# Where the load of layer 1's first value weights stands in SyncE's queue, in a two-layer attention kernel

## The chip, the cores and the metric

The kernel runs on one core of a Trainium2 chip. The metric is the device time of one execution in microseconds (us). Everything is fp32.

## What is computed

The input is 4 images of 16x16 pixels with 1024 channels, that is, 1024 tokens of 1024 features. Two layers follow each other, of which only the seam matters here:

```python
x = x + _L0_conv_ref(_gn(x), ...)        # layer 0: linear attention, content and position parts
t = _to_tokens(x)
t = t + _L1_attn_ref(_ln_t(t), ...)      # layer 1: qkv = einsum('btc,oc->bto', ln, W_attn) + b_attn, 16 heads
t = t + _L1_ffn_ref(_ln_t(t), ...)       # 8 gated experts
```

In layer 0 the content part and the position part add up to a matrix that is multiplied with the values: `Y = Yc + Yp`. The result is added to `x`, the tokens are normed over their features (`_ln_t`), and layer 1 starts with its value projection, which multiplies the normed tokens with the last third of `W_attn`.

## The kernel before

Tokens are worked on in 8 tiles of 128 (`NT`). At the seam the tiles come in the order of `tiles` (L569): second halves of the four images first (t = 1, 3, 5, 7), then the first halves (0, 2, 4, 6). The loop at L615 takes them one after the other, under a manual schedule, so that each engine runs its instructions in the order of the program. A step of it does this for tile i:

- `spread(i)` (L583): TensorE makes the content products of tile i+1 (`pc`, L444), VectorE adds them to the attention matrix `s` (L452); TensorE multiplies `s` with the values (`py`, L595) and VectorE adds that to `x` (L602).
- `layer_norm` (L184): VectorE takes the statistics, ScalarE writes the normed rows into one of three slots of `ln_rows` (L162).
- `turn_quarters(i - 2)` (L605): VectorE transposes the quarters of the tile before last into `ln1`, features on partitions (L179).
- `turn_by_rows` (L202): SyncE (SP) writes the normed rows to DRAM (L204), and four DMAs read them back as quarters (`quarters_of`, L174), which the transpose above takes two steps later.
- GpSimd adds `b_proj` to `x` and stores the rows to `x_rows` from its own queue (L629, L630).

The last two tiles don't go through DRAM: TensorE transposes them (`turn_on_pe`, L207). Tile 6 is normed in the loop, tile 7 (tile numbers are places in the order) after it.

All DMAs of SP stand in one queue in program order. Ahead of the loop stand 88 copies that move the position part from `two_T` to `s` (L479), and then the load of `w_v0`, 2 MB: the first half of layer 1's value weights, features by 512 columns. It is a `w_tile` (L115) from a pool of two buffers; the buffer that it gets held the key and value weights of layer 0 (`w_kv`). Its readers come after the loop: `first(0, 1)` and `first(0, 3)` on TensorE (L656, called at L710), and the sums `sums_v(0, nc.gpsimd)` on GpSimd (L152 to L155, called at L709). The second half, `w_v1` (L729), goes to the buffer of `ln_rows` once tile 7 has been transposed.

The value products that follow take the tiles of `ln1` by token: `first(0, 1)` and `first(0, 3)` need tiles 0 and 1 of the order, `first(0, 0)` (L719) needs tile 4 (t = 0), and `first(0, 2)` (L723) needs tile 5 (t = 2). PSUM has three banks with the tag `mm` and three with the tag `tr`; a product that takes a bank waits until the last reader of what was there has finished.

Of the kernel before, what the change touches and what calls it, by code (L numbers as in the profile page):

```python
# [40 lines left out]
C = 1024  # L41
# [16 lines left out]
HALF = 512  # L58
# [11 lines left out]
def kernel(  # L70
# [44 lines left out]
    def w_tile(name, *parts, home=None, queue=nc.sync):  # L115

        w = (home or wpool).tile([P, NC, HALF], F32, tag="w", name=name)
        at = 0
        for part in parts:
            n = part.shape[1]  # L120
            queue.dma_start(w[:, :, at : at + n], part.rearrange("(c p) n -> p c n", p=P))
            at += n
        return w
# [47 lines left out]
    def quarters_of(rows, row):  # L171

        for f in range(Q):
            nc.sync.dma_start(row[ts(f, 32), :, :], rows[:, f, :].rearrange("(g j) c -> j g c", j=32))  # L174
        return row
# [8 lines left out]
    def layer_norm(ln, t, on_pe=False):  # L184


        stats = small.tile([P, 2, 6], F32, tag="ln_stats", name=f"ln1_stats{t}")
        for j in range(2):
            nc.vector.bn_stats(stats[:, j, :], xs[t][:, ts(j, HALF)])
        mv = small.tile([P, 2], F32, tag="ln_mv", name=f"ln1_mv{t}")  # L190
        nc.vector.bn_aggr(mv, stats)
        rstd = small.tile([P, 1], F32, tag="ln_rstd", name=f"ln1_rstd{t}")
        inverse_root(rstd, mv[:, 1:2], EPS)
        if on_pe:
            less = small.tile([P, 1], F32, tag="ln_less", name=f"ln1_less{t}")
            nc.vector.scalar_tensor_tensor(less, mv[:, 0:1], -1.0, rstd, ALU.mult, ALU.mult)
            for j in range(2):
                nc.scalar.activation(ln[:, ts(j, HALF)], xs[t][:, ts(j, HALF)], AF.Identity, bias=less, scale=rstd)
            return
        normalised(ln, xs[t], mv[:, 0:1], rstd)  # L200

    def turn_by_rows(ln, t, quarters, turns):  # L202
        rows = turns.tile([P, Q, C // Q], F32, tag="rows", name=f"ln1_rows{t}")
        nc.sync.dma_start(rows.rearrange("n f c -> n (f c)"), ln)  # L204
        quarters_of(rows, quarters)
# [13 lines left out]
    with ExitStack() as layer0:  # L219
# [363 lines left out]
        def spread(i):  # L583
            b, nt = tiles[i]
            t = 2 * b + nt
            if i == 0:
                content(b, nt)
            if i + 1 < NT:
                content(*tiles[i + 1])
            for hp in range(2):  # L590
                py = mm(f"py{t}_{hp}")
                for hl in range(2):
                    bh = b * HEADS0 + 2 * hp + hl
                    for mh in range(2):
                        nc.tensor.matmul(  # L595
                            py[:, ts(hl, M)],
                            s0[:, mh, ts(nt, S2), :, bh].rearrange("p i j -> p (i j)"),
                            v_T[:, mh, ts(b, M)],
                            start=(mh == 0),
                            stop=(mh == 1),  # L600
                        )
                nc.vector.tensor_add(xs[t][:, ts(hp, HALF)], xs[t][:, ts(hp, HALF)], py)  # L602
            return t

        def turn_quarters(i):  # L605
            of, quarters = to_turn[i]
            turn(ln1[:, :, ts(of, P)], quarters)
# [2 lines left out]
            of[:, :C].rearrange("p (f c) -> p f c", f=Q)  # L610
            for of in (emb.rearrange("p c i j -> p (c i j)"), s_w.rearrange("p a c n -> p (a c n)"))
        ]
        w_v = [w_tile("w_v0", W_attnT[:, 2 * C : 2 * C + HALF])]
        in_order.enter_context(tc.manual_schedule())
        for i in range(NT - 1):  # L615
            t = spread(i)
            quarters = None
            if i < NT - 2:
                if i < NT - 4:
                    quarters = spare[i % 2]  # L620
                else:
                    quarters = late.tile([P, Q, C // Q], F32, tag="xg", name=f"ln1_quarters{t}")
            to_turn.append((t, quarters))
            layer_norm(ln_rows[:, i % 3, :], t, i >= NT - 2)
            if i >= 2:
                turn_quarters(i - 2)
            if i < NT - 2:
                turn_by_rows(ln_rows[:, i % 3, :], t, quarters, turns)
                nc.gpsimd.tensor_add(xs[t], xs[t], bp)  # L629
                nc.gpsimd.dma_start(x_rows[ts(t, P), :], xs[t])  # L630
            else:
                nc.sync.dma_start(x_rows[ts(t, P), :], xs[t])
# [1040 lines left out]
```

## Time and profile before

| What | Value |
|---|---|
| Time, median of 3 runs | 1248.14 us (1246.36 to 1249.39) |
| Time of the profiled execution | 1246.09 us |
| Its span | 1244.2 us |
| Busy: TensorE (PE) | 1221.8 us, 98% |
| Busy: VectorE (DVE) | 740.5 us, 60% |
| Busy: GpSimd (POOL) | 409.1 us, 33% |
| Busy: ScalarE (ACT) | 219.9 us, 18% |
| Mean granted TensorE clock | 0.995 |
| HBM read, written | 116.12 MB, 48.50 MB |

A page of the profile gives, for one execution, the busy time of each engine; the span in 40 equal slices, with the busy share in tenths (9 is 90% or more) and the granted clock of TensorE (PEclk) in tenths; the waits, each with what ended it; and the chain of work that ended last. A line of the timeline has the start in us, the duration in us, the engine, the line of the kernel, the operation with output and input and the number of instructions, and in brackets the idle time before it and what ended that. SPq stands for SyncE's queue of DMA issues: its duration is the issue, not the transfer. Times are us from the start of the span.

### The profile page before, as it was taken

What the parts mean: (1) busy time and instruction counts of PE and PEld (TensorE: products, weight loads), DVE (VectorE), ACT (ScalarE), POOL (GpSimd) and SP (SyncE); (2) the same over time, 40 slices, a digit from 0 to 9 for tenths busy, and PEclk for the clock granted to TensorE, in tenths of its full rate; (3) what the DMA queues carried; (4) which work ended last, traced back from release to release, by engine and by line L of the source; (5) the groups of instructions that cost most, each with busy time, mean ns of one, the idle gap of its engine ahead of it and who ended that gap; (6) DMA issues with size and microseconds to landing.
All of it is one profiled execution on the core that took longest, in us unless ns stands there. A gap on an engine that the chain in (4) does not pass through costs nothing.

```text
span 1244.2 us, 13333 instructions
## 1 busy us (share of the span) xinstructions
PE 1221.8 (98%) x4796; PEld 632.7 (51%) x4796; DVE 740.5 (60%) x1333; ACT 219.9 (18%) x514; POOL 409.1 (33%) x470
## 2 busy tenths in 40 slices
PE   9999999799999999999999999999999999999998
PEld 5445885578884444444444444444344434434443
DVE  5796636477332666657554866765656656565642
ACT  3310111121000222223121422110210111111110
POOL 0041341246000222222232115445552745363521
PEclk9999999899999999999999999999999999999999
DMA  9002025862202535353383657383856485656442
GB/s 350 20 1 85 1 52 155 261 210 69 68 1 68 155 103 160 107 169 107 102 288 117 209 203 255 72 234 91 240 126 176 103 235 154 155 129 190 100 84 54
DMA packets 94121, 169.77 MB, mean 136 GB/s; under 512 B 11968, under 2 KB 48848, under 8 KB 94048
## 3 DMA queue, kind: packets, MB, share of 16 engines
q1 hardware_dynamic: 75680, 112.68, 27.8%
q0 software_dynamic: 16144, 51.45, 17.3%
q10 hardware_dynamic: 2224, 4.72, 1.1%
q8 instruction: 40, 0.66, 0.2%
q14 instruction: 33, 0.27, 0.1%
HBM read 116.12 MB, written 48.50 MB: 132 GB/s over the span
## 4 chain that ended last, share of the span: by engine, by line
PE 73%; issue 13%; POOL 5%; DVE 3%; DMA 3%; SPq 2%; ACT 1%; POOLq 0%; DVEq 0%; ACTq 0%
PE p L1440 31%; PE pv L656 8%; PE po L897 6%; POOL s_q L854 5%; PE pq_pair L392 4%; PE left L1482 3%; PE pq L311 3%; PE pqk L656 3%; PE pk L423 2%; PE rest L1496 2%; PE pv L530 2%; PE pT L502 2%; SPq L479 1%; DMA s<-two_T 1%; DMA ln_rows<-ln_rows 1%
## 5 line engine op out<-in xcount | busy, mean ns | idle before, releaser
L1009 POOL DMA_INDIRECT w_e_xg<-rows,gather x146 | 157.1, 1076 | 57.3 <-issue 40.2
L1440 PE MATMUL p<-w_e,A 128*128 128x512 f32 x368 | 163.2, 593 | 1.3 <-DVE slot L1275 1.3
L854 POOL TENSOR_TENSOR s_q<-s_q,total 128x128 f32<-128x128 f32 (+1 forms) x128 | 66.2, 548 | 275.5 <-DVE total L851 273.1
L897 PE MATMUL po<-w_p,y_T 128*128 128x512 f32 x256 | 118.5, 604 | 0.0
L1440 PEld LDWEIGHTS p<-w_e,A 128*128 128x128 f32 x368 | 69.6, 190 | 89.9 <-issue 89.2
L1032 POOL DMA_INDIRECT out_dram<-y,add x32 | 56.6, 1768 | 176.9 <-ACT y L1446 113.0
L1440 PE MATMUL p<-T,S 128*128 128x512 f32 x256 | 112.7, 593 | 0.0
L1446 ACT ACTIVATE y<-y,slot 128x512 f32<-128x512 f32 x64 | 46.1, 722 | 332.5 <-DVE y L1454 177.6
L840 ACT ACTIVATE s_q<-s,top 128x256 f32<-128x256 f32 (+1 forms) x128 | 56.6, 443 | 186.3 <-issue 146.8
L656 PE MATMUL pqk<-ln,w_qk 128*128 128x512 f32 x192 | 85.6, 595 | 0.0
L1440 PEld LDWEIGHTS p<-T,S 128*128 128x128 f32 x256 | 48.6, 190 | 60.8 <-issue 60.5
L897 PEld LDWEIGHTS po<-w_p,y_T 128*128 128x128 f32 x256 | 45.9, 190 | 47.9 <-issue 46.9
L179 DVE STREAM_TRANSPOSE A<-w_e_xg 128x1024 f32<-128x1024 f32 x32 | 39.6, 1238 | 49.6 <-DMA w_e_xg<-rows,gather 47.6
L656 PE MATMUL pqk<-T,S_qk 128*128 128x512 f32 x128 | 58.5, 599 | 0.0
L656 PEld LDWEIGHTS pqk<-ln,w_qk 128*128 128x128 f32 x192 | 36.0, 190 | 43.3 <-issue 42.1
L1440 PE MATMUL p<-T,A 128*128 128x512 f32 x128 | 57.5, 592 | 0.0
L1440 PE MATMUL p<-w_e,S 128*128 128x512 f32 x128 | 57.5, 592 | 0.0
L311 PE MATMUL pq<-w_q,xn 128*128 128x512 f32 x96 | 44.5, 599 | 0.3 <-ACT xn L291 0.3
L656 PE MATMUL pv<-w_v,ln 128*128 128x256 f32 x192 | 43.5, 380 | 0.2 <-ACT ln L215 0.2
L1482 PE MATMUL left<-w_e,one 128*32 128x512 f32 x312 | 41.8, 593 | 0.0
L1440 PEld LDWEIGHTS p<-T,A 128*128 128x128 f32 x128 | 24.3, 190 | 30.6 <-issue 30.1
L1440 PEld LDWEIGHTS p<-w_e,S 128*128 128x128 f32 x128 | 24.3, 190 | 30.6 <-issue 30.1
(327 smaller groups left out, 1895.6 us busy)
## 6 DMA issues: line engine op xcount, KB each, us to landing
w_e<-in_expert_w_dram SPq DMA_DIRECT2D x14, 2048.0 KB, 15.4
s_rows<-s_q SPq DMA_DIRECT2D x32, 384.0 KB, 2.3
s_rows<-s_rows SPq DMA_DIRECT2D x128, 96.0 KB, 2.4
w_qk<-in_W_attnT_dram SPq DMA_DIRECT2D x8, 1024.0 KB, 5.6
xn<-in_xT_dram SPq DMA_DIRECT2D x8, 512.0 KB, 5.5
w_q<-in_Wq_dram SPq DMA_DIRECT2D x16, 256.0 KB, 7.7
x_at<-in_x_dram POOLq DMA_DIRECT2D x8, 512.0 KB
w_v<-in_W_attnT_dram SPq DMA_DIRECT2D x2, 2048.0 KB
```

What stands on the lines that cost most here:

```text
L179: nc.vector.transpose(row_T[:, :, :slots].rearrange("p c (g j) -> p g c j", j=32), row[:, : slots // 32, :].rearrange("p g (c i) -> p g c ...
L311: nc.tensor.matmul(pq, xn[:, c, ts(t, P)], w_q[kc][:, c, :], start=(c == 0), stop=(c == NC - 1))
L392: nc.tensor.matmul(bank, a[:, c, :], b[:, c, :], start=(c == 0), stop=(c == NC // 2 - 1))
L656: nc.tensor.matmul(bank, stationary(c), moving(c), start=(c == 0), stop=(c == NC // 2 - 1))
L840: nc.scalar.activation(blocks(h, qt), s[:, h, cols].rearrange("p (b f i) -> p b f i", f=Q, i=32), AF.Exp, bias=top[:, qt, h : h + 1], accu ...
L854: nc.gpsimd.tensor_mul(blocks(h, qt), blocks(h, qt), total[:, qt, h : h + 1].unsqueeze(2).unsqueeze(3).to_broadcast([P, 1 + qt, Q, 32]),)
L897: nc.tensor.matmul(po, y_T[:, c, ts(t, P)], w_p[j][:, c, :], start=(c == 0), stop=(c == NC - 1))
L1009: nc.gpsimd.indirect_dma_start(out=row[:, g, :], out_offset=None, in_=table[: (TOK - P) * Q, :] if e in SHORT else table, in_offset=bass.I ...
L1032: nc.gpsimd.indirect_dma_start(out=out[: TOK - P, :] if e in SHORT else out, out_offset=bass.IndirectOffsetOnAxis(ap=add[:slots, e, k : k ...
L1440: nc.tensor.matmul(bank, a[:, c, :], b[:, c, :], start=(c == 0), stop=(c == NC // 2 - 1))
L1446: nc.scalar.mul(y[i][:, ts(j, HALF)], y[i][:, ts(j, HALF)], slot[:, e, 1, 2 * pair + i : 2 * pair + i + 1])
L1482: nc.tensor.matmul(bank[ts(i, 32), :], stationary, w[of][j][:, c, :], start=(c == 0), stop=(c == NC - 1))
```

## The change

The line that allocates `w_v0` and issues its load is taken from its place ahead of the loop and put into the loop, in step i = 3, behind `turn_by_rows` of that tile. In SP's queue the load then stands behind the rows and the four quarters of the fourth tile and in front of the rows of the fifth. The buffer, the size and the readers of the load stay the same, and so does every other instruction.

```diff
@@ -610,7 +610,6 @@
             of[:, :C].rearrange("p (f c) -> p f c", f=Q)
             for of in (emb.rearrange("p c i j -> p (c i j)"), s_w.rearrange("p a c n -> p (a c n)"))
         ]
-        w_v = [w_tile("w_v0", W_attnT[:, 2 * C : 2 * C + HALF])]
         in_order.enter_context(tc.manual_schedule())
         for i in range(NT - 1):
             t = spread(i)
@@ -626,6 +625,8 @@
                 turn_quarters(i - 2)
             if i < NT - 2:
                 turn_by_rows(ln_rows[:, i % 3, :], t, quarters, turns)
+                if i == 3:
+                    w_v = [w_tile("w_v0", W_attnT[:, 2 * C : 2 * C + HALF])]
                 nc.gpsimd.tensor_add(xs[t], xs[t], bp)
                 nc.gpsimd.dma_start(x_rows[ts(t, P), :], xs[t])
             else:
```

## The prediction

> **What bounds the kernel now.** I read the page first. The slices are 31.1 us long.
>
> ```profile
> PE   9999999799999999999999999999999999999998
> PEclk9999999899999999999999999999999999999999
> ```
>
> TensorE is full in every slice except the eighth (217.7 to 248.8 us) and the last, and in the eighth its clock dips too. So only a stall of PE there has much to give back. That slice is the loop at L615. Next, the waits from 200 to 310 us (waiter, releaser, us in total, times, longest).
>
> ```profile
> DVE ln L179 <- DMA ln_rows<-ln_rows: 10.6, 1, 10.6
> ...
> PE pc L444 <- DVE s L452: 8.5, 1, 8.5
> ```
>
> VectorE waited once, 10.6 us, for a DMA behind the first transpose, and PE waited 8.5 us for VectorE. The timeline says which transfer it was.
>
> ```profile
> 226.40 0.53 SPq L121 DMA_DIRECT2D w_v<-in_W_attnT_dram  x1
> 227.03 0.52 SPq L204 DMA_DIRECT2D ln_rows<-ln_rows  x1
> ...
> 238.45 2.33 SPq L174 DMA_DIRECT2D emb<-ln_rows  x4
> 240.87 0.38 SPq L204 DMA_DIRECT2D ln_rows<-ln_rows  x1
> 244.73 1.73 SPq L174 DMA_DIRECT2D s_w<-ln_rows  x4
> ```
>
> The 2 MB load goes out at 226.40 and tile 0's rows (0.5 MB) right behind it. Their quarters can't be read back before the rows have landed, at 238.4, 11.4 us after issue; the next tile's rows, with no load in front, go from 240.87 to 244.7. What that holds up:
>
> ```profile
> 244.06 1.25 DVE L179 STREAM_TRANSPOSE ln<-emb 128x1024 f32<-128x1024 f32 x1 [10.60 <-DMA ln_rows<-ln_rows]
> ...
> 245.93 4.63 PE L444 MATMUL pc<-q,k_q 128*128 128x512 f32 x5 [8.51 <-DVE s L452]
> ...
> 249.51 2.90 PE L444 MATMUL pc<-q,k_q 128*128 128x512 f32 x4
> ```
>
> PE ended tile 3's products at 237.43 and needs the `s` additions that queue behind the transpose on VectorE. A content of eight matmuls otherwise takes 3.43 us start to start (230.32 to 233.75); this one took 245.93 to 252.25, since its clock had fallen. Five-us stretches show it (us; busy PE, PEld, DVE, ACT, POOL; granted clock; DMA share; GB/s):
>
> ```profile
> 235.00:240.00 5.00, 2.43 (x12) 2.13 (x10) 0.00 (x0) 0.00 (x0) 2.73 (x2) 1.00 0.65 246
> 240.00:245.00 5.00, 0.00 (x0) 0.00 (x0) 0.94 (x1) 0.00 (x0) 0.00 (x0) 0.63 0.70 210
> 245.00:250.00 5.00, 4.07 (x5) 1.85 (x6) 4.61 (x12) 0.20 (x1) 0.00 (x0) 0.50 0.68 210
> ```
>
> From 250 on PE is busy without a break to 285, and the chain that ended last then stays on PE to 408.
>
> **What the Trainium skill says.** "DMA: Bandwidth & Descriptors", section "Queues, rings and completion order": one engine consumes descriptors of a queue in ring order. The trace agrees: 11.4 us for rows behind the load, 2.6 to 3.8 for other rows. The same page, "Anatomy of one DMA": a semaphore wait is made by the issuing sequencer, not by the DMA engines, so what stands behind a waiting instruction on SP isn't issued. The trace agrees: SP waited for rows six times at L174, 25.3 us in all. "TensorE: Matmul & The Clock Gate", "The HAM clock gate": an idle window of some 3.4 us halves the clock, and a busy one restores it. The trace agrees: idle from 237.4, clock 0.66 in 241 to 242, then 0.50.
>
> **The change, part by part.**
>
> *Removed: the load ahead of tile 0's rows.* SP is busy with the `s<-two_T` copies until 226.3, so the rows go out at 226.4, not sooner, although they were ready at 220.8. They land 2.6 to 3.2 us later, say 3.0: 229.4. Four quarter issues take 2.33 (as at 238.45; 1.73 elsewhere): 231.8. Before, the last ended at 240.78 and the transpose began at 244.06, 3.3 later; so 235.1. VectorE wants it at 233.46 and still waits 1.6 us. PE doesn't feel that: it needs the first `s` addition by 237.43, which is one transpose (1.17 to the next start) and one addition (0.65) after 235.6. With landings as long as the longest shown (4.3) PE would lose about 0.8; with the shortest, nothing. I take nothing. PE then does tile 4's products at 237.43+3.43 = 240.86, not 252.25: **11.4 us** (8.5 idle, 2.9 slow clock), all on the path.
>
> *SP between.* A tile costs SP some 3.0+2.3 = 5.3 us against PE's 7.0 a tile (219.78 to 226.77), so SP catches up: rows 1 at 231.8, quarters landed by 240.3 (wanted at 240.5); rows 2 at 237.1, rows 3 at about 242.4, landed 245.4, quarters issued by 247.4. The buffers that these wait for (turn 0 and turn 1) come free at 236 and 242. No PE time.
>
> *Added: the load behind tile 3's quarters.* Issue at 247.4, 0.5 us of SP, hidden, because rows 4 are normed only at 248.85. It needs w_kv's buffer, last read by 206. From the first case, load plus rows took 226.40 to 238.38, 12.0 us, with row stores beside it. Alone, the second half of these weights took 8.1:
>
> ```profile
> 285.71 0.38 SPq L121 DMA_DIRECT2D w_v<-in_W_attnT_dram  x1
> ...
> 293.80 3.28 POOL L152 TENSOR_TENSOR s_v<-w_v 128x1024 f32<-128x1024 f32 x1 [8.11 <-DMA w_v<-in_W_attnT_dram]
> ```
>
> So the load is there between 255.5 and 258.5. Its readers come at 273.28 (PE, L656) and 273.54 (GpSimd, L152) in the old trace, 11.4 earlier 261.9 and 262.1. Cover of at least 3 us; each us beyond it would cost one.
>
> *What queues behind it: rows 4 and 5.* Rows 4 land at 247.4+12.0 = 259.4 instead of some 251.5. Quarters: +2.33+3.3 = 265.1. Turn 4 is wanted at 272.91-11.4 = 261.5, so **VectorE waits about 3.6 us there**. Behind it on VectorE are tile 7's additions and norm; PE has its four first products meanwhile (7.07 us, already fed). PE needs tile 7 normed for the transposes at 284.51-11.4 = 273.1. From turn 4's start to that norm's end took 4.0 us to its variance, then about 2.4 for root, inverse, shift and two ScalarE halves: limit 266.7. Slack 1.6 us. Its other need, the matmul banks that tile 7's additions free for L719, falls at 267.7. Rows 5 then go out at 261.8, quarters landed by 270.5; turn 5 must start by about 272.4 (1.2 for itself, 0.7 for two additions before PE's products at 285.79-11.4 = 274.4). Slack 1.9. Both unshown landings are bounded: best, with the load in 8.1 and 1.7 for the rows, turn 4 waits 2; worst, with the load at the 206 GB/s that the traffic had in 250 to 255, rows come 4.8 later (2.1 MB in 10.2 us against 5.4 at 390 GB/s, the rate in 288 to 293) and PE loses 3.2. A gain is excluded: nothing waited for rows 4. I take no loss of PE, and 0.2 for small misfits.
>
> *Nothing else moves.* Row stores are on GpSimd's queue, with no new wait. The second half's load still waits for tile 7's transposes and goes 11 us earlier with them.
>
> Sum: -11.4+0.2 = **-11.2 us**. The profiled execution took 1246.09 (span 1244.2, 1.9 around it); it gives 1234.9. That run is 2.05 under the median of the three, which I shift alike: 1248.14-11.2 = 1236.9.
>
> **Rivals.**
>
> *The stall moves to turn 4.* The load stands in front of a row again. For: the wait is certain, and its slack to PE only 1.6 us. Against: PE has four products in hand, which it hadn't at turn 0. If rows come the 4.8 later, PE idles 3.2, too short to lose the clock: 1240.1.
>
> *It was not the load.* The 4 MB of `x_at` and the `s` copies fill the engines up to 226, and rows 0 might be late because of them. Then the wait stays: 1248.1. Against: 2 MB of load plus 0.5 of rows plus stores make up the about 400 GB/s that ran from 229 to 237, and at 227 to 228 the rate had fallen to 43.
>
> *Slower: the load becomes the late one.* Place: PE's first product at L656, 261.9. Each us that it lands later idles PE one; it eats the whole gain from a landing at 273.3, and the result is slower by over 0.2% from 275.8, 28 us after issue. At 30 us: +4.1, 1252.2. Against: 12 us is the worst seen for load and rows together.
>
> **How the numbers follow.** Forecast 0.64, moved stall 0.27, not the load 0.05, late load 0.04. 0.2% (2.5 us) is about what a measurement of this kernel can tell from no change. The first two are both faster, 0.91; same 0.05; slower 0.04. Range: the three runs spread -1.8 to +1.2; from 1235.2 (a full 11.4 with a run 1.5 below) to 1241.0 (moved stall and 0.9), leaving out about 0.17.
>
> **What would show it.** Right: rows 0 issued at 226.4 and landing within 4 us; no PE wait near 237; PEclk 1.00 throughout 235 to 255; the load issued at 246 to 249; a VectorE wait of 2 to 5 us before turn 4 and none of PE over 1 us. Wrong: a wait of L444 on `s` that remains, PE waiting at L211 or L719 or with its first product on w_v, or a turn 5 later than 272.

## The result, and the profile after

The changed kernel takes 1238.5 us (median of 4 runs, 1237.3 to 1241.1) against 1248.5 for the kernel before on the same chip: the medians lie 10.0 us apart, and the ratio of the means is 0.9925 with a 95% interval of 0.9904 to 0.9946, that is, 6.7 to 12.0 us less. Two later comparisons of the same pair on other chips gave ratios of 0.9947 (0.9932 to 0.9962; medians 5.8 us apart) and 0.9933 (0.9919 to 0.9947; 8.0 us). The forecast was 11.2 us. The profiled execution after took 1237.34 us, with a span of 1235.5 against 1244.2.

The same two lines of the page after: the eighth digit of PE and of its clock is 9 now.

```profile
PE   9999999999999999999999999999999999999998
PEclk9999999999999999999999999999999999999999
```

The waits after, from 200 to 310 us. VectorE's one wait of 10.6 us at the transposes has become two short ones and one of 6.0, and PE's 8.5 us at L444 are gone. PE now waits 1.1 us, for ScalarE, at the value products that take tile 5 (`first(0, 2)`, now at L657).

```profile
DVE ln L179 <- DMA ln_quarters<-ln_rows: 6.9, 2, 6.0
...
DVE ln L179 <- DMA emb<-ln_rows: 1.4, 1, 1.4
```

The timeline after (start, duration, engine, line, operation, and in brackets the idle time before it):

```profile
226.58 0.53 SPq L204 DMA_DIRECT2D ln_rows<-ln_rows  x1
229.58 1.88 SPq L174 DMA_DIRECT2D emb<-ln_rows  x4
...
235.08 1.25 DVE L179 STREAM_TRANSPOSE ln<-emb 128x1024 f32<-128x1024 f32 x1 [1.40 <-DMA emb<-ln_rows]
...
237.49 3.60 PE L444 MATMUL pc<-q,k_q 128*128 128x512 f32 x8
...
250.10 0.40 SPq L121 DMA_DIRECT2D w_v<-in_W_attnT_dram  x1
250.60 0.52 SPq L204 DMA_DIRECT2D ln_rows<-ln_rows  x1
...
262.59 2.36 SPq L174 DMA_DIRECT2D ln_quarters<-ln_rows  x4
...
267.55 1.25 DVE L179 STREAM_TRANSPOSE ln<-ln_quarters 128x1024 f32<-128x1024 f32 x1 [5.97 <-DMA ln_quarters<-ln_rows]
...
275.58 0.70 PE L657 MATMUL pv<-w_v,ln 128*128 128x256 f32 x2 [1.05 <-ACT ln L215]
```

Tile 0's rows land 2.9 us after their issue, and tile 4's products follow tile 3's without a gap. The long wait stands in front of rows 4 now: 250.60 to 262.6. VectorE pays 6 us for it, PE one.

### The profile page after: what moved, and what is told of

The parts are those of the page before. It is cut to its first block, busy times and chain, and to the rows that moved or that the text cites. A ratio compares the mean times of both kernels' runs of the same rounds, so it can differ in the third digit from the quotient of the medians.

```text
span 1235.5 us, 13332 instructions
## 1 busy us (share of the span) xinstructions
PE 1219.3 (99%) x4796; PEld 631.7 (51%) x4796; DVE 740.5 (60%) x1333; ACT 219.8 (18%) x514; POOL 409.6 (33%) x470
## 4 chain that ended last, share of the span: by engine, by line
PE 70%; issue 13%; POOL 5%; DMA 4%; DVE 4%; SPq 2%; ACT 1%; POOLq 0%; DVEq 0%; ACTq 0%
PE p L1441 31%; PE pv L657 7%; PE po L898 6%; POOL s_q L855 5%; PE pq_pair L392 4%; PE left L1483 3%; PE pq L311 3%; PE pqk L657 3%; PE pk L423 2%; DMA ln_rows<-ln_rows 2%; PE rest L1497 2%; PE pv L530 2%; PE pT L502 2%; SPq L479 2%; DMA s<-two_T 1%
## 5 line engine op out<-in xcount | busy, mean ns | idle before, releaser
L657 PE MATMUL pqk<-ln,w_qk 128*128 128x512 f32 x192 | 85.6, 595 | 0.0
L657 PE MATMUL pqk<-T,S_qk 128*128 128x512 f32 x128 | 58.5, 599 | 0.0
L657 PEld LDWEIGHTS pqk<-ln,w_qk 128*128 128x128 f32 x192 | 36.0, 190 | 43.3 <-issue 42.3
L657 PE MATMUL pv<-w_v,ln 128*128 128x256 f32 x192 | 43.5, 380 | 1.1 <-ACT ln L215 1.1
## 6 DMA issues: line engine op xcount, KB each, us to landing
w_v<-in_W_attnT_dram SPq DMA_DIRECT2D x2, 2048.0 KB, 11.2
```

What stands on the lines that cost most here:

```text
L657: nc.tensor.matmul(bank, stationary(c), moving(c), start=(c == 0), stop=(c == NC // 2 - 1))
```

## What the experiments test

In what follows, rows n are the write of tile n's normed rows to DRAM, quarters n the four reads back, and turn n VectorE's transpose of them. My theory: a load in front of a tile's rows makes that tile's transpose some 9 us late; PE stalls by what isn't covered, and loses clock with it; only turn 4 has four value products in hand that cover it. Rivals: that any place behind tile 0's rows is as good; that the queue's order is the cause, so that a queue of its own for the load would free the rows; that the clock is no part of the loss; and that traffic in all, not the order, makes the stall.

All runs in one table. The second column is the difference to the kernel before on the same chip (medians, with the 95% interval); the third is what PE waited between 226 and 300 us; the fourth the start of the query products, the first work that no longer hangs on the seam. It was 372.2 us in the kernel before; without its 8.5 us of waiting at L444 and 2.9 of slow clock it would be 360.8. The last column is what remains of the fourth after 360.8 and the waits: the clock, and small things.

| Kernel | us against before | PE waits, us | queries start | rest |
|---|---|---|---|---|
| before | 0 | 8.5 (L444) + 0.2 | 372.2 | 2.7 |
| changed, first comparison | -10.0 (-12.0 to -6.7) | 1.1 (L657) | 362.0 | 0.1 |
| r_after | -5.8 (-8.5 to -4.7) | 1.7 + 0.5 + 1.1 | 364.7 | 0.6 |
| r_after2 | -8.0 (-10.1 to -6.6) | 1.0 + 0.5 + 1.1 | 364.0 | 0.6 |
| step2 | -1.5 (-3.6 to -0.7) | 1.2 + 4.6 + 0.2 | 368.6 | 1.8 |
| step4 | -4.1 (-5.1 to -2.7) | 5.5 | 367.6 | 1.3 |
| act3 | -5.1 (-6.2 to -3.0) | 3.1 + 0.2 | 365.9 | 1.8 |
| half0 | -5.4 (-7.4 to -4.0) | 4.2 + 0.2 | 367.6 | 2.4 |
| split34 | -2.2 (-3.5 to -1.2) | 1.1 + 8.1 | 372.9 | 2.9 |
| xlate | -3.2 (-4.7 to -2.1) | 3.6 + 0.9 | 366.9 | 1.6 |
| warm | +2.2 (1.0 to 3.0) | 13.9 of added work | 374.4 | -0.3 |
| warm8 | -1.6 (-2.4 to -0.7) | 6.9 of added work + 1.7 + 0.2 | 369.5 | -0.1 |
| late_stores | -8.0 (-10.5 to -7.1) | 0.2 + 2.2 | 363.3 | 0.1 |
| late_stores_before | +1.4 (0.0 to 2.1) | 5.9 + 2.2 + 0.2 | 373.3 | 4.2 |

Single executions of one kernel differ by 1 to 6 us, and the waits are those of one profiled execution each; so the trace says where the time went, and the medians how much. Medians are compared with the kernel before on the same chip; r_after, step2, step4 and act3 ran on one chip, warm, half0, split34 and xlate on a second, and r_after2, warm8 and the two with late stores on a third.

## The changed kernel again (r_after, r_after2)

No edit. The expectations on record:

> The changed kernel again, beside the kernel before on the same chip, as the yardstick for the others. Theory (the load stood in front of tile 0's rows in one queue; behind tile 3's quarters nearly all of its wait is covered): 9 to 11 us below the kernel before, about 1238.5, with VectorE waiting about 6 us before turn 4 and PE about 1 us before tile 5's products at L657. Rival (part of the 10 us is chance in the gating stage): the gain at the end differs from that at 380 us by more than 1 us, in either direction.

> The changed kernel once more, as the yardstick for the three beside it. Theory (its gain is 11.4 us less what PE waits at three places: at L444 for turn 0, at L211 and L657 for turn 4 and 5, and the first of these varies with rows 0, which took 2.9 us in one execution and 4.7 in another): 5 to 10 us below the kernel before, and what PE waits at the seam, taken from 11.4, gives the gain of the seam within 1 us. Rival (the variation lies in later stages): the seam's end stands as in the first trace of the changed kernel and the total differs by 2 us or more.

In r_after rows 0 went out at 227.55 and landed 4.7 us later, not 2.9; turn 0 came at 237.5, past the limit of 235.6 that the prediction had worked out, and PE waited.

```profile
227.55 0.53 SPq L204 DMA_DIRECT2D ln_rows<-ln_rows  x1
...
232.23 1.79 SPq L174 DMA_DIRECT2D emb<-ln_rows  x4
...
237.50 1.25 DVE L179 STREAM_TRANSPOSE ln<-emb 128x1024 f32<-128x1024 f32 x1 [3.75 <-DMA ln_rows<-ln_rows]
...
239.37 1.12 PE L444 MATMUL pc<-q,k_q 128*128 128x512 f32 x2 [1.65 <-DVE s L452]
```

So PE waited 1.7 us at L444, 0.5 at L211 and 1.1 at L657. Taken from 11.4 that is 8.1 us; the queries began 7.5 us sooner than before. In r_after2 the same sum is 8.8 against 8.2. Both keep the theory's margin of 1 us, but the 9 to 11 us that I had expected of r_after in all were a miss: it gained 5.8. The gain up to the queries isn't a constant: it is 11.4 less what the waits at three tight places take, and the prediction's own slacks there are 0.5 us (turn 0), 1.6 (turn 4) and 1.9 (turn 5). At the end of the span the three profiled executions gain 8.7, 5.9 and 6.9 us, each 1.3 to 1.6 less than at the queries: so r_after's rival has a part in it too, and the section on the prediction comes back to that.

## Another place in SP's queue (step2, step4)

```diff
-                if i == 3:
+                if i == 2:        # step2; step4 has 4
                     w_v = [w_tile("w_v0", W_attnT[:, 2 * C : 2 * C + HALF])]
```

> The load behind the third tile's quarters, so in front of the rows of tile 3. Theory (a load in front of rows costs about 9 us at the turn that takes them; only turn 4 has PE work in hand that covers it): load issued at about 244.5, rows 3 land at 257, quarters by 262.6, VectorE waits 8 us before turn 3, PE waits about 6 us at L595 for the additions behind it and loses its clock as well, 2 to 3 us: 7 to 9 us over the changed kernel, about 1246.5. Rival (all that matters is that tile 0's rows go first, any later place is as good): within 1.5 us of the changed kernel, 1238.5.

> The load behind the fifth tile's quarters, so in front of the rows of tile 5. Theory: rows 4 no longer wait (landing within 4 us, turn 4 at 261.5 without a wait), but the load is issued at about 255.7 and lands 8.1 to 10.3 later, 263.8 to 266.0; PE wants it at 262.0 and waits 2 to 4 us for it; turn 5 comes at 273.6, hidden behind that. Net 1 to 3 us over the changed kernel, about 1240.5. Rival (the remaining loss is turn 4's wait, and the load has cover enough): 1 us below the changed kernel, 1237.5.

The timeline of step2, where the load stands in front of rows 3:

```profile
262.51 1.25 DVE L179 STREAM_TRANSPOSE ln<-s_w 128x1024 f32<-128x1024 f32 x1 [6.74 <-DMA s_w<-ln_rows]
...
264.39 5.42 PE L595 MATMUL py<-v_T,s 128*128 128x256 f32 x16 [4.61 <-DVE s L452]
```

The stall of the kernel before comes back three turns later, with a slow clock too (5.42 us for 16 matmuls that otherwise take 3.7). The kernel is 4.3 us above the changed one on the same chip: the 7 to 9 expected were too much. The wait for turn 3 was 6.7 us and not 8, PE's at L595 4.6 and not 6, and the changed kernel had 3.3 us of waits of its own on that chip. "Any later place will do" is refuted.

In step4 rows 4 land 3.5 us after issue and turn 4 needs no wait, as expected, but the load comes too late for PE:

```profile
255.83 0.40 SPq L121 DMA_DIRECT2D w_v<-in_W_attnT_dram  x1
...
267.38 2.93 PE L657 MATMUL pv<-w_v,ln 128*128 128x256 f32 x6 [5.52 <-DMA w_v<-in_W_attnT_dram]
```

It was there 11.5 us after issue, not 8.1 to 10.3, so PE waited 5.5 us: this is the prediction's third rival, the late load, on the chip. The wait is longer than the 2 to 4 us expected. The medians put step4 1.7 us above the changed kernel on that chip, within the 1 to 3 expected, since the changed kernel there had other waits; their intervals overlap, so this difference isn't clear of noise. Of the three places tried, step 3 has the lowest median: one earlier has no cover for the transpose, one later none for the load.

## Its own queue (act3)

```diff
-                    w_v = [w_tile("w_v0", W_attnT[:, 2 * C : 2 * C + HALF])]
+                    w_v = [w_tile("w_v0", W_attnT[:, 2 * C : 2 * C + HALF], queue=nc.scalar)]
```

> The load at the same place of the loop, but issued by ScalarE on its own queue, at about 242.3. Theory (rows wait because descriptors of one queue are taken in order): rows 4 land within 4.5 us of their issue, turn 4 and turn 5 come without a wait over 1 us, PE's wait of 1.05 us is gone; rows 3 and quarters 2 share the engines with the load and come 1 to 2 us later, inside their slack. About 1 us below the changed kernel, 1237.5. Rival (the 16 engines' rate is what delays rows, whatever the queue): the rows issued while the load runs take 8 us or more, a turn waits 4 us or more, and the time is the same as that of the changed kernel or above it, 1238.5 to 1241.

The rival was right. The load went out at 240.93 on ScalarE's queue, 1.6 us ahead of the quarters of tile 2 on SP's:

```profile
240.93 0.42 ACTq L121 DMA_DIRECT2D w_v<-in_W_attnT_dram  x1
...
242.52 1.85 SPq L174 DMA_DIRECT2D emb<-ln_rows  x4
...
244.47 0.39 SPq L204 DMA_DIRECT2D ln_rows<-ln_rows  x1
...
252.80 1.25 DVE L179 STREAM_TRANSPOSE ln<-emb 128x1024 f32<-128x1024 f32 x1 [5.25 <-DMA emb<-ln_rows]
...
253.89 1.90 SPq L174 DMA_DIRECT2D s_w<-ln_rows  x4
```

From the last issue to the transpose quarters 2 took 8.4 us (3.3 in the kernel before), and rows 3 landed after 9.4, without standing behind the load in any queue. The queues from 243 to 247 us in the same run (packets, MB, share of the 16 engines; q10 carries the load, q1 is SP's) show who was served:

```profile
q10 hardware_dynamic: 699, 1.43, 96.9%
q1 hardware_dynamic: 63, 0.06, 5.0%
```

The load held the engines almost alone. The prediction had leaned on the Trainium skill, "DMA: Bandwidth & Descriptors", section "Queues, rings and completion order". That section also says that each engine takes turns between the queues that have work, packet by packet. That isn't what this window shows: the queue that came first had 97% of the engines' time for 4 us. What does agree is the same page's section "Issuing engines are not separate DMA queues": DMAs from several issuing engines run on the same 16. So order in one queue is one way to stand behind a big transfer, and not the only one; the 11.4 us of the kernel before fit the rule of ring order that the prediction cited, but don't show that rule to be the cause. The run changes the time of the load too, not only its queue: ScalarE issued it 9 to 11 us sooner than SP does in the changed kernel, so other rows stood behind it. The time is that of the changed kernel on that chip or a little above (1241.6 against 1240.9).

## Half the load (half0, split34)

```diff
+        w_v0 = []
+
+        def w_v0_part(j):
+            if not w_v0:
+                w_v0.append(wpool.tile([P, NC, HALF], F32, tag="w", name="w_v0"))
+            rows = W_attnT[j * 4 * P : (j + 1) * 4 * P, 2 * C : 2 * C + HALF]
+            nc.sync.dma_start(w_v0[0][:, 4 * j : 4 * j + 4, :], rows.rearrange("(c p) n -> p c n", p=P))
...
+        w_v0_part(0)                  # half0: ahead of the loop, and in it
                 if i == 3:
-                    w_v = [w_tile("w_v0", W_attnT[:, 2 * C : 2 * C + HALF])]
+                    w_v0_part(1)
...
-                if i == 3:            # split34: only in the loop
-                    w_v = [w_tile("w_v0", W_attnT[:, 2 * C : 2 * C + HALF])]
+                if i in (3, 4):
+                    w_v0_part(i - 3)
...
+        w_v = [w_v0[0]]               # both: behind the loop
```

> The load in two halves of 1 MB: features 0 to 511 in front of tile 0's rows, as the kernel before has the whole, and features 512 to 1023 behind tile 3's quarters, as the changed kernel has the whole. Theory (what stands in front costs its bytes at the engines' rate): tile 0's rows land some 5.5 us after their issue and not 11.4, VectorE waits 4 to 6 us before turn 0, PE 2 to 4 us at L444 with most of its clock kept, and turn 4 has no wait over 3 us: 5 to 8 us below the kernel before. Rival (a load in front costs a wait for its completion whatever its size): rows 0 still take 9 us or more, 0 to 3 us below the kernel before.

> The load in two halves of 1 MB: features 0 to 511 behind tile 3's quarters, features 512 to 1023 behind tile 4's. Theory (turn 4's wait is the bytes in front of rows 4, and the load has some 3 us of cover): rows 4 land 5 to 7 us after their issue and not 12, turn 4 waits 1 us or less, and the second half, issued at about 257 to 259, lands at 263 to 265, when PE's second product wants it at 263.7 to 265.6; rows 5 come in front of turn 5's limit. PE's waits at L211 and L657 fall to under 1 us in all: 0.5 to 1.5 us below the changed kernel on the same chip, which was at 1240.9. Rival (the wait only moves on to turn 5 and to the second half's product): same as the changed kernel within 1 us, or above.

The timeline of half0:

```profile
240.48 1.25 DVE L179 STREAM_TRANSPOSE ln<-emb 128x1024 f32<-128x1024 f32 x1 [6.30 <-DMA emb<-ln_rows]
...
242.35 5.40 PE L444 MATMUL pc<-q,k_q 128*128 128x512 f32 x8 [4.21 <-DVE s L452]
```

Half the bytes in front of rows 0 halve the stall: 4.2 us of waiting against 8.5, with rows 0 landing 7.7 us after issue against 11.4. That puts the stall on the bytes in front and not on some fixed wait; the landing came 2 us later than expected. That most of the clock would be kept was a miss: the eight products took 5.40 us instead of 3.60, and the rest in the table is 2.4 us.

In split34 the same half did little good. Rows 4 took 10.1 us with 1 MB in front, against 12.5 with 2 MB. And SP, which may not issue quarters 4 before rows 4 have landed, held the second half behind them until 264.3; it landed 8.9 us later, with PE waiting 8.1 us and its clock down to 0.50:

```profile
PE pv L666 <- DMA w_v<-in_W_attnT_dram: 8.1, 1, 8.1
```

The theory's 390 GB/s failed there: between 252 and 262.3 the engines moved only 279 GB/s, at times 100. This split gains 2.2 us over the kernel before, where the changed kernel gained 5.8 to 10.0 on other chips, and the rival was the better of the two expectations.

## The other transfers at the seam (xlate, late_stores, late_stores_before)

```diff
-        for b, nt in tiles:           # xlate
+        for b, nt in tiles[:4]:
             t = 2 * b + nt
             nc.gpsimd.dma_start(xs[t], x[ts(t, P), :])
...
                 nc.gpsimd.dma_start(x_rows[ts(t, P), :], xs[t])
+                if i < 4:
+                    b, nt = tiles[i + 4]
+                    nc.gpsimd.dma_start(xs[2 * b + nt], x[ts(2 * b + nt, P), :])
```

```diff
-                nc.gpsimd.dma_start(x_rows[ts(t, P), :], xs[t])      # late_stores, on the kernel after;
...                                                                   # late_stores_before, on the one before
         sums_v(0, nc.gpsimd)
+        for b, nt in tiles[: NT - 2]:
+            nc.gpsimd.dma_start(x_rows[ts(2 * b + nt, P), :], xs[2 * b + nt])
```

> The changed kernel, with the loads of x for tiles 4 to 7 of the order not in one row ahead of the loop but one by one in steps 0 to 3, on GpSimd's queue behind the row stores. Theory (what is left of turn 0's wait, 1.4 to 3.7 us, comes from the x loads that share the engines with the s copies up to 222 us and so put off rows 0): the s copies end 2 to 4 us sooner, rows 0 go out at 222 to 225, turn 0 has no wait and PE none at L444; the loop then carries 0.5 MB a step more and rows may take 1 to 2 us longer, so that turn 4 waits 1 to 2 us more. 0 to 2 us below the changed kernel on the same chip. Rival (SP's own issue time sets when rows 0 go out): rows 0 at 226 or later all the same, and the time the same or 1 to 3 us above, as the rows get slower.

> The changed kernel, with the six row stores to x_rows (0.5 MB each, GpSimd's queue) not in the loop but all behind the sums of the first value weights on GpSimd. Theory (rows, quarters and the load wait for the 16 engines' time, whatever the queue): rows and quarters land about 1 us sooner, the load and rows 4 in about 10 us instead of 12, turn 0 waits 1.5 us or less, turn 4 under 5 us, and PE's waits at the seam fall under 0.5 us in all; the stores then run at 272 to 284, beside the second half's load, which has 25 us of slack to PE. 1 to 4 us below the changed kernel. Rival (the stores cost nothing where they are): same as the changed kernel within 1 us; or above it, if VectorE's sums of B must wait for the stores to leave x's place by more than the 4 us that PE has in hand.

> The same move of the six row stores, but with the load where the kernel before has it, in front of tile 0's rows. Theory (the 2 MB in front decide, the stores add only the 0.5 to 1 MB that run beside them): rows 0 land about 10 us after their issue instead of 11.4, PE still waits 6 to 8 us at L444 and loses its clock: 1 to 3 us below the kernel before, and 5 us or more above the late stores with the load behind tile 3. Rival (traffic in all, not the order of load and rows, makes the stall): within 3 us of the late stores with the load behind tile 3.

In xlate rows 0 do go out sooner, at 223.9, but then take 4.9 us and their quarters longer still, and PE waits 3.6 us before tile 4: -3.2 us against the kernel before, less than any of the three comparisons of the changed kernel, where 0 to 2 us more had been expected. The x loads now go out among the rows and quarters; that they are what slows them fits, but wasn't tested apart.

Late stores do at the seam what was expected: load and rows 4 take 10.4 us instead of 12.5, and PE waits 0.2 us up to the end of the first products. Then the rival's case comes in, as VectorE's sums write where x lay:

```profile
DVE T L686 <- DMA x_rows<-x_at: 6.0, 1, 6.0
...
PE pv L656 <- DVE T L687: 2.2, 1, 2.2
```

The 2.2 us given back make it equal to the changed kernel on that chip (1237.98 and 1237.95). With the load in its old place, the same move leaves 5.9 us of PE's wait and ends 9.4 us above the late stores with the load behind tile 3:

```profile
PE pc L444 <- DVE s L452: 5.9, 1, 5.9
```

The place of the load decides, and the traffic of the stores is second; that rival is refuted. The 1 to 3 us below the kernel before that I expected of it didn't come: +1.4 us, from the 2.2 us at the sums and a second fall of the clock there.

## The clock (warm, warm8)

```diff
         in_order.enter_context(tc.manual_schedule())       # on the kernel before
+        warm = ps.tile([P, 2, HALF], F32, tag="sc", name="warm", bufs=1)
         for i in range(NT - 1):
             t = spread(i)
+            if i == 3:
+                for _ in range(8):                          # warm: 16
+                    nc.tensor.matmul(warm[:, 0, :], v_T[:, 0, :P], v_T[:, 0, :HALF], start=True, stop=True)
```

> The kernel before (load in front of tile 0's rows), with 16 further matmuls of 128x512 on TensorE between tile 3's products and tile 4's, into a bank that nobody reads: 6.9 us of work in the 8.5 us in which PE stood idle. Theory (8.5 us of the seam's loss are waiting, 2.9 us the clock that falls with it): the wait for the additions at L452 ends when it did, the clock stays at 1.00, tile 4's products take 3.4 us and not 6.3: 2 to 3 us below the kernel before. Rival (the clock is no part of it, or the loss is made good later): same as the kernel before, within 1 us.

> The kernel before with 8 further matmuls of 128x512 in PE's idle time. The earlier run had 16, and each is two records of 0.43 us, so that they took 13.9 us and not 6.9: PE was at tile 4's products 5.6 us later than before, and yet the time was only 2.2 us over the kernel before. Now 8 of them take 6.9 us and end at about 244.3, before the additions come at 246. Theory (2.9 us of the loss are the clock): clock 1.00 throughout, 2 to 3 us below the kernel before. Rival (the 3.4 us that the earlier run got back came from elsewhere): within 1 us of the kernel before.

The first run missed its purpose: the 16 matmuls took 13.9 us, 5.4 more than the gap, and my expectation had counted half. It still told something: PE's next content products (L444) began at 251.50, 5.6 us later than before, and the queries only 2.2. In warm8 PE has 6.9 us of idle work and waits 1.7 on top, as long as before in all, with its clock at 1.00: the queries begin 2.7 us sooner, and the time falls by 1.6 us (0.7 to 2.4). A stretch of five us of warm8 (us; busy PE, PEld, DVE, ACT, POOL; granted clock; DMA share; GB/s):

```profile
245.00:250.00 5.00, 3.99 (x11) 2.18 (x12) 4.63 (x11) 0.20 (x1) 0.00 (x0) 1.00 0.64 210
```

The kernel before had a clock of 0.50 in this stretch. So the clock is a cost of its own beside the wait. The trace puts it at 2.7 us against the prediction's 2.9; the median, 1.6, is less than the 2 to 3 expected.

## Why the prediction was right, step by step

**Rows 0 and turn 0: right, but tighter than I wrote.** Issue 226.58 (said 226.4), landing after 2.9 us (3.0), turn 0 at 235.08 (235.1), waiting 1.4 us (1.6); tile 4's products at 240.92 (240.86). I took no loss of PE here, though, and two of three profiled executions had one, 1.7 and 1.0 us. The bound that I gave for long landings, 0.8 us, was the right term and too small: r_after's rows took 4.7 us, not 4.3, and went out a us later.

**SP between: the term that was mis-sized.** I had 5.3 us of SP for a tile; it took 6.3 from rows 1 to rows 2 and 6.6 from rows 2 to rows 3, as rows 1 to 3 land after 3.7 to 4.8 us instead of the 3.0 that I took. The trace before already had 3.7 to 3.9 for these three; only rows 4 and 5 landed after 2.6. So the load was issued at 250.10, not 247.4 and outside the 246 to 249 that I had named as a sign.

**Load and rows 4: right together, lucky for the load.** 12.5 us together against 12.0, only 2.7 us later. But the load alone landed 11.2 us after its issue, where I had given 8.1 to 11.1, and so at 261.3 against the 261.97 at which PE took it (said 261.9). The cover that I had put at 3 us or more was 0.7; in r_after and r_after2, where the load took 11.5 us, it was 0.2 and nothing. The late load, which I had given 0.04, was closer than I thought, and step4 shows its price.

**Turn 4: the moved stall, in small.** At 267.55 instead of 265.1 it passed the limit of 266.7 by 0.9 us, and PE waited 1.05 us, by the path that the prediction named: tile 7's norm, its transposes at 273.20, ScalarE's copies. So the forecast's zero was wrong and the first rival's mechanism came true at a third of its 3.2 us. Turn 5 came at 273.14, past my limit of 272.4. The profile puts PE's wait to ScalarE's copies, but VectorE's additions behind turn 5 ended at the same time within 0.1 us, so turn 5 may have a part in the 1.05 us. One reason that I gave against that rival is wrong: 3.2 us of idling isn't too short to lose the clock. In act3 PE waited 3.1 us and the clock fell to 0.50 (columns as in warm8):

```profile
256.00:258.00 2.00, 2.00 (x4) 0.85 (x3) 1.93 (x5) 0.00 (x0) 0.00 (x0) 0.50 0.99 325
```

**The sum.** At the seam 372.2 - 362.0 = 10.2 us against 11.2 forecast; the missing 1.0 is that wait. The profiled pair differs by only 8.7: the other 1.5 us went in the stage of layer 1's gates, which took 17.7 us from the first to the last product of L1025 instead of 16.1 at L1024. A copy there came late, in after:

```profile
752.58 0.29 DVE L1165 COPY sums<-parts 128x128 f32<-128x128 f32 x1 [5.67 <-PE dense_pe L1025]
```

and in before:

```profile
761.96 0.29 DVE L1164 COPY sums<-parts 128x128 f32<-128x128 f32 x1 [4.83 <-PE parts L1162]
```

The first follows its products (750.47) by 2.1 us, the second (760.70) by 1.3. It is not shown to be chance: the three profiled executions of the changed kernel took 17.7, 17.7 and 16.9 us in this stage, step2 19.4 and step4 17.0, and the other nine of the table's kernels 16.0 to 16.2. The prediction's "nothing else moves" leaves this out; the cause wasn't tested and stays open. In medians the first comparison, on which the forecast was right, is the best of the three: r_after gained about half of the 11.2 us.

**What stays open.** Why the engines serve the earlier big load almost alone isn't settled by act3. Why the gate stage is longer in the changed kernel isn't known. And a version that keeps both gains, with some of the stores late but not all of them, wasn't tried.

## What to carry to other kernels

Before a bulk load goes out, ask who waits for what is issued in the next ten us, and put the load where that consumer has other work in hand; 2 MB in front of half a MB made it some 8 to 9 us late in the same queue (11.4 to 12.5 us against 2.6 to 4.8), and some 5 us or more from another queue (9.4 in act3). A stall of TensorE is priced as the wait plus the clock: here 8.5 + 2.7. And slacks of under 2 us are no cover but a spread of the result: the same change brought the queries forward by 7.5, 8.2 and 10.2 us. The medians gained 5.8, 8.0 and 10.0, but their intervals overlap, and how much of that spread is the chips' isn't shown.

## What I had not expected of the hardware

PE's clock fell after a wait of 2.2 us in one run and not after one of the same length in another. In late_stores_before PE waited 2.16 us up to 295.56, and then (stretches of 2 us; columns as above, the granted clock third from the end):

```profile
294.00:296.00 2.00, 0.44 (x2) 0.42 (x3) 1.97 (x3) 0.00 (x0) 0.00 (x0) 1.00 1.05 284
296.00:298.00 2.00, 2.00 (x7) 1.61 (x6) 2.00 (x3) 0.00 (x0) 0.61 (x1) 0.57 0.13 49
298.00:300.00 2.00, 2.00 (x7) 1.60 (x6) 2.00 (x1) 0.00 (x0) 1.98 (x1) 0.58 0.00 0
```

In late_stores it waited 2.15 us up to 287.26, at the same instruction:

```profile
286.00:288.00 2.00, 0.74 (x3) 0.68 (x4) 2.00 (x2) 0.00 (x0) 0.00 (x0) 1.00 0.92 266
288.00:290.00 2.00, 2.00 (x11) 1.75 (x10) 2.00 (x3) 0.00 (x0) 0.93 (x1) 1.00 0.06 22
```

The Trainium skill, "TensorE: Matmul & The Clock Gate", section "The HAM clock gate", says that the window in which activity is judged is free-running, so that it depends on where in it one falls. That may be why the two runs differ, though no run shows the window itself. But the same section asks for an idle window of some 3.4 us before the clock falls, and here 2.16 us were enough, as were 3.1 in act3; the measurement decides. Over the table, waits up to 1.7 us left the clock at 1.00, a wait of 3.1 us and more went with a rest of 1.3 to 2.9 us (4.2 in late_stores_before, which had two), and 2.2 us did either.
